# A decoder layer on one core: the last but one group's shared expert placed behind the expert tiles, and two long GpSimd instructions of each group cut in four

## The chip, the cores and the metric

The kernel runs on one core of a Trainium2 chip. The metric is the device time of one execution in microseconds (us). The core's engines are TensorE (PE in the profile, its weight loads PEld), VectorE (DVE), ScalarE (ACT), GpSimd (POOL) and SyncE (SP, which here issues DMAs).

## The reference, cut to what matters

The layer works on 32 batches of 112 tokens with 256 features, with a context of 375 rows for each batch:

```python
x = x + delta_attention(layernorm(x))            # rmsnorm, delta-rule scan over the tokens, and an MLP
x = x + cross_attention(layernorm(x), context)   # 16 heads of 16 features, mask over 375 context rows
xt = layernorm(x)                                # 3584 rows
probs = sigmoid(xt @ gate_w.T + gate_b)          # 6 experts
w, idx = top_k(probs, 2); w = w / (sum(w) + 1e-8)
y = sum over experts e:  w_e * ((silu(xt @ ew1[e].T) * (xt @ ew3[e].T)) @ ew2[e].T)
z = (silu(xt @ fc1.T) * (xt @ fc2.T)) @ fc3.T    # the shared expert, every row
x = x + y + z
```

Inside the delta attention, `h = rmsnorm(x) * norm1_w` gives queries, keys and values, and `beta = sigmoid(h @ beta_w + beta_b)`, one number for each token. Its output is `x + attn @ Wo + mlp(rmsnorm(x + attn @ Wo))`, to which the layer's own residual is added.

## The kernel before, in words

The 32 batches are worked off as eight groups (`groups`) of four (`GB = 4`); T is 112 tokens and D 256 features. A group passes three stages: the delta attention (`delta_block`, L693, and `queries`, together `ahead(g)`), the cross-attention in quads of four heads (`scores`, `turned`, `product`, then `cross_out`), and the feed-forward part with six experts. Stages of neighbouring groups are interleaved: while the quads of group g run, the delta attention of group g+1 and the feed-forward work of an earlier group fill the time between them.

**The delta attention.** `delta_block` begins with a layernorm into `h`, ScalarE making the four batches one after another. `hb = h * nwb` (L702; the profile calls its buffer `u`) is one instruction of 112x1024, on VectorE for group 0 and on GpSimd for all others; `beta` is reduced from it. Towards its end `nc.gpsimd.tensor_tensor(xt, xt, x1, ALU.add)` (L912, `x<-x,u` in the profile) adds the attention's part to the residual, again one instruction of 112x1024. Its second operand `x1` lies in a buffer with the tag `u`, which VectorE fills in two halves.

**The feed-forward part.** For groups 0 to 6, `mixture_sparse` (L1189) normalizes, turns the rows into features, computes the gate (`route`), and scatters every row twice, once for each of its two experts, into a table `rows` in DRAM (`dispatch`, `place_row`, L1144: eight indirect DMAs a group on GpSimd). It then runs the shared expert (`shared`: fc1, fc2, fc3) and stores the sum `acc` to `kept[g]`. `acc` is the group's tile `x_of[g]`. When group 6 is dispatched, `tables`, `gather` and `sparse_tiles` run the experts over 54 tiles of 128 rows: GpSimd gathers `xg` from `rows`, TensorE transposes it, multiplies up (L1327) and down (L1344), and SP stores `y` to `results` in DRAM. The last group, 7, does not pass through the tables: `mixture_dense` computes all six experts for its rows. Beside that, `combine` (L1370) finishes groups 0 to 6: for each, one load of `kept` on SP, and eight gathers from `results` on GpSimd (two for each batch), which VectorE multiplies by the weights and adds. Every gather reads `results` as a whole, so the first waits for the last store to it. The three buffers of a group in `combine` are taken in turn from nine `homes`, buffers that earlier stages have left.

**What sets the order.** The operations aren't issued at once: a `Recorder` notes them (so most have L381, the line of its replay), and its list scheduler `flush` writes out the order of TensorE, VectorE and ScalarE by hand, with costs from `price`. GpSimd and SP work off their queues in the order that this gives. Dependencies between engines are semaphores that the tile framework sets. The tail of the main function is

```python
    for _ in range(2):
        next(tiles)
    drain(out_of)
    dense = mixture_dense(groups - 1, x_of[groups - 1])
    next(dense)
    drain(tiles)
    rest = combine()
    next(rest)
    for _ in dense:
        next(rest, None)
```

In the profile `bank` is a PSUM bank, `nT` and `hT` are feature-major activations, `w_Wk` and `w_Wq` weights of the delta attention, and `mk` a buffer with this tag that also holds short-lived things, such as the copy of `rs` to 112x256.

## Time and profile before

| | us |
|---|---|
| median of 3 runs | 1423.21 |
| lowest, highest | 1422.33, 1423.34 |
| the profiled execution | 1423.09 |
| its span, first to last instruction | 1421.2 |
| outside its span | 1.9 |
| mean granted TensorE clock | 0.984 |
| TensorE busy | 1357.0 |
| VectorE busy | 970.9 |
| ScalarE busy | 704.3 |
| GpSimd busy | 308.1 |

A line of the timeline reads: start, duration, engine, line, operation, output and inputs with their shapes, and in brackets the idle time of the engine before it and what ended that. A line of a table by windows reads: the stretch and its length, then for PE, PEld, DVE, ACT and POOL the busy time with the number of instructions, then the granted clock, the share of DMA and its rate. A line of the waits names the waiting engine and buffer, the releaser, the total, the number of times and the longest.

The groups are regular: from 376.57 on, TensorE starts the same matmuls (`bank<-nT,w_Wk`) of the next group every 142 to 144 us, the last time at 946.41. The cross-attention of the last group goes on to about 1162, the tiles of the experts from 1162 to 1340, and the dense group with `combine` from there to the end.

### The profile page before, as it was taken

The page shows a single profiled execution, that of the slowest core. Times are in us where ns is not written, and L with a number is a line of the kernel's source. Part 1 is how long each engine was busy: PE and PEld are TensorE (multiplying, and loading weights), DVE is VectorE, ACT ScalarE, POOL GpSimd, SP SyncE. Part 2 cuts the span into 40 slices and gives each one's busy share as a digit, 9 for nine tenths or more (in the row PEclk, how much of TensorE's full clock was granted, in tenths as well). Part 3 has the DMA queues.
Part 4 walks back from the last instruction along what each step waited for, and adds up shares of the span by engine and source line. Part 5 has one row for each costly group of instructions (what it writes and reads, how often), then busy time and mean ns, then how long its engine had stood idle before and what let it go on. Part 6 is the DMA issues. An engine that isn't in the chain of part 4 may idle for free.

```text
span 1421.2 us, 26865 instructions
## 1 busy us (share of the span) xinstructions
PE 1357.0 (95%) x9700; PEld 919.6 (65%) x9700; DVE 970.9 (68%) x3171; ACT 704.3 (50%) x1946; POOL 308.1 (22%) x477
## 2 busy tenths in 40 slices
PE   6689999999999999999999999999999999999996
PEld 4456766776577657765776577667767666666653
DVE  6646766866886588668866786577757875455575
ACT  2124756654565456545654565466547673222110
POOL 2131000420041104100420041103110122223275
PEclk9779999999999999999999999999999999999999
DMA  9200100123012301230123012301225122222255
GB/s 259 79 8 14 35 17 17 36 69 94 17 36 69 94 17 36 69 94 16 37 69 94 17 37 68 94 17 37 61 76 163 38 64 76 85 89 84 66 169 153
DMA packets 95077, 94.76 MB, mean 67 GB/s; under 512 B 29921, under 2 KB 89057, under 8 KB 94945
## 3 DMA queue, kind: packets, MB, share of 16 engines
q1 hardware_dynamic: 86816, 72.71, 17.8%
q0 software_dynamic: 8128, 20.34, 4.8%
q8 instruction: 77, 1.26, 0.4%
q14 instruction: 56, 0.45, 0.1%
HBM read 50.90 MB, written 42.12 MB: 65 GB/s over the span
## 4 chain that ended last, share of the span: by engine, by line
PE 78%; DVE 9%; ACT 6%; issue 2%; DMA 2%; POOL 1%; POOLq 0%; DVEq 0%; ACTq 0%
PE bank L381 68%; PE bank L1327 7%; PE bank L1344 3%; ACT e L381 3%; ACT eT L381 1%; ACT h L381 1%; DVE mk L381 1%; DMA e<-results,row_i 1%; DVE W L381 1%; DVE rs_u L381 1%; DVE rs_i L381 1%; DVE ms L381 1%; DVE x L381 1%; DVE nT L381 1%; DVE qz L381 1%
## 5 line engine op out<-in xcount | busy, mean ns | idle before, releaser
L381 ACT ACTIVATE e<-e,nmx 112x375 f32<-112x375 f32 x512 | 306.2, 601 | 193.9 <-DVE nmx L381 192.8
L381 DVE CUSTOM_DVE_ANT_0 e<-bank,neg,flip 112x375 f32<-112x375 f32 x512 | 282.4, 604 | 41.5 <-PE bank L381 37.1
L381 ACT COPY eT<-bank 125x448 f32<-125x448 f32 x384 | 187.3, 529 | 90.1 <-PE bank L381 86.3
L381 PEld LDWEIGHTS bank<-ident,e 112*125 112x125 f32 x1536 | 186.6, 188 | 32.6 <-issue 9.6
L381 PE MATMUL bank<-ident,e 112*125 112x112 f32 x1536 | 201.7, 276 | 1.0 <-ACT e L381 0.7
L381 PE MATMUL bank<-kx,qz 32*112 32x375 f32 x1024 | 120.8, 518 | 0.0
L1327 PE MATMUL bank<-ew,xT 128*128 x216 | 101.9, 595 | 1.0 <-ACT e L381 1.0
L381 PEld LDWEIGHTS bank<-eT,vx 125*32 125x32 f32 x3072 | 69.2, 109 | 50.9 <-issue 37.2
L381 PE MATMUL bank<-eT,vx 125*32 125x112 f32 x3072 | 100.2, 263 | 1.3 <-DVE nT L381 1.3
L381 PE MATMUL bank<-w_xwvT,cT 128*125 128x256 f32 x384 | 100.4, 388 | 0.0
L381 DVE SCALAR_TENSOR_TENSOR hs<-hs,bank 128x256 f32<-128x256 f32 x108 | 45.4, 421 | 77.7 <-ACT hs L381 75.9
L1144 POOL DMA_INDIRECT rows<-h,row_i x56 | 52.6, 940 | 210.5 <-DMA rows<-blank 91.3
L381 ACT ACTIVATION_READ_ACCUMULATOR e<-e,nmx 112x1 f32 x512 | 96.8, 189 | 0.0
L381 PE MATMUL bank<-cT,w_xwkT 128*128 128x375 f32 x256 | 95.4, 498 | 0.0
L381 POOL DMA_INDIRECT xg<-rows,take x54 | 51.6, 955 | 130.7 <-PE bank L381 121.4
L381 ACT ACTIVATE hs<-bank 128x256 f32<-128x256 f32 x54 | 20.7, 384 | 116.2 <-PE bank L1327 113.0
L381 PEld LDWEIGHTS bank<-w_xwvT,cT 128*125 128x125 f32 x384 | 66.9, 187 | 12.0 <-issue 4.6
L381 DVE SCALAR_TENSOR_TENSOR qk<-qk,bank 128x448 f32<-128x448 f32 x56 | 34.8, 621 | 56.6 <-ACT qk L381 48.9
L381 POOL TENSOR_TENSOR u<-h,nwb 112x1024 f32<-112x1024 f32 x7 | 16.8, 2399 | 244.8 <-issue 235.3
L381 PEld LDWEIGHTS bank<-kx,qz 32*112 32x112 f32 x1024 | 40.4, 169 | 40.6 <-issue 18.7
L381 PEld LDWEIGHTS bank<-cT,w_xwkT 128*128 128x128 f32 x256 | 44.1, 190 | 33.0 <-issue 7.1
L381 DVE TENSOR_TENSOR x<-x,bank 112x512 f32<-112x512 f32 (+1 forms) x64 | 35.2, 550 | 33.5 <-PE bank L381 33.2
(245 smaller groups left out, 2406.5 us busy)
## 6 DMA issues: line engine op xcount, KB each, us to landing
rows<-blank SPq DMA_DIRECT2D x42, 448.0 KB
cT<-in_ctxT_dram SPq DMA_DIRECT2D x32, 375.0 KB
results<-y SPq DMA_DIRECT2D x54, 128.0 KB
mk<-in_mask_dram SPq DMA_DIRECT2D x32, 164.1 KB
x<-in_x_dram SPq DMA_DIRECT2D x7, 448.0 KB
kept<-x SPq DMA_DIRECT2D x7, 448.0 KB
out_dram<-x SPq DMA_DIRECT2D x4, 448.0 KB
blocks<-W SPq DMA_DIRECT2D x8, 196.0 KB
```

The lines of the kernel that those rows point to most:

```text
L381: getattr(getattr(self.nc, name), op)(*[real(a) for a in args], **{k: real(v) for k, v in kwargs.items()})
L1144: sent = rec.nc.gpsimd.indirect_dma_start(out=rows[:], out_offset=bass.IndirectOffsetOnAxis(ap=where, axis=0), in_=row, in_offset=None)
L1327: rec.nc.tensor.matmul(p.real(), xT[:, c, :], w13[:, bass.ds(at[i] * (NC * 2 * MI) + c * 2 * MI, 2 * MI)], start=(c == 0), stop=(c == NC - 1),
L1344: rec.nc.tensor.matmul(p[:, :D].real(), hT[:, c, :], w2[:, bass.ds(at[i] * (CH * D) + c * D, D)], start=(c == 0), stop=(c == CH - 1),)
```

## The change

It has three parts. First, the two GpSimd instructions of 112x1024 in `delta_block` (`hb` for groups 1 to 7, the add of `x1` for all eight) are written as four instructions of 112x256, one for each batch. Secondly, for group 6 (`groups - 2`) `mixture_sparse` issues all the scatters at once and leaves the shared expert and the store of `kept[6]` to a new function `keep_shared`, which the main function drains behind the tiles and before `combine`; the other groups run it where they did. Thirdly, because `x_of[6]` lives longer by that, the order of the `homes` is changed: the buffer with the tag `x`, first before, is now the last of the nine.

```diff
@@ delta_block
         hb = dlt.tile([T, GB, D], F32, tag="u", name=f"hb_{g}")
-        plain.tensor_tensor(hb, h, over_batches(nwb), ALU.mult)
+        if g == 0:
+            nc.vector.tensor_tensor(hb, h, over_batches(nwb), ALU.mult)
+        else:
+            for b in range(GB):
+                nc.gpsimd.tensor_tensor(hb[:, b, :], h[:, b, :], nwb, ALU.mult)
...
-        nc.gpsimd.tensor_tensor(xt, xt, x1, ALU.add)
+        for b in range(GB):
+            nc.gpsimd.tensor_tensor(xt[:, b, :], xt[:, b, :], x1[:, b, :], ALU.add)
@@ mixture_sparse
-        yield from shared(g, acc, aT, lambda: next(places, None))
+        if g == groups - 2:
+            yield from places
+            owed.append((g, acc, aT))
+        else:
+            yield from keep_shared(g, acc, aT, lambda: next(places, None))
+
+    owed = []
+
+    def keep_shared(g, acc, aT, first=lambda: None):
+        yield from shared(g, acc, aT, first)
         nc.sync.dma_start(out=kept[g].rearrange("b t d -> t b d"), in_=acc)
@@ combine
         homes = [
             pool.tile([T, GB, D], F32, tag=tag, bufs=bufs)
-            for pool, tag, bufs, n in ((io, "x", 3, 1), (att, "e", 3, 3), (att, "eT", 2, 2), (feat, "qz", 2, 2))
+            for pool, tag, bufs, n in ((att, "e", 3, 3), (att, "eT", 2, 2), (feat, "qz", 2, 2), (io, "x", 3, 1))
             for _ in range(n)
-        ] + [scratches[0].rearrange("p (b d) -> p b d", b=GB)[:T]]
+        ]
+        homes.insert(-1, scratches[0].rearrange("p (b d) -> p b d", b=GB)[:T])
@@ main
     dense = mixture_dense(groups - 1, x_of[groups - 1])
     next(dense)
     drain(tiles)
+
+    drain(keep_shared(*owed[0]))
     rest = combine()
```

## The prediction

> **What bounds the kernel now.** The page's busy totals come first, then the waits of TensorE by releaser.

> ```profile
> PE 1357.0 (95%) x9700; PEld 919.6 (65%) x9700; DVE 970.9 (68%) x3171; ACT 704.3 (50%) x1946; POOL 308.1 (22%) x477
> ...
> PE bank L381 <- DVE nT L381: 10.2, 14, 1.5
> ```

> TensorE is busy 95% of the span, so time comes from its idle gaps, from its clock, or from work behind its end. Of the 10.2 us that it waits for `nT`, five gaps of about 1.5 us are one event, once a group (376.57, 518.85, 660.80, 802.75, 946.41). The timeline around the second, on all engines:

> ```profile
> 515.28 2.41 POOL L381 TENSOR_TENSOR u<-h,nwb 112x1024 f32<-112x1024 f32 x1 [42.72 <-issue]
> 515.34 2.50 DVE L381 COPY mk<-rs 112x256 f32<-112x256 f32 x1
> ...
> 517.77 0.34 DVE L381 TENSOR_SCALAR neg<-mk 112x375 f32<-112x375 int32 x1
> 518.03 0.67 DVE L381 TENSOR_SCALAR nT<-bank,v_norm_w 128x448 f32<-128x448 f32 x1
> ```

> VectorE's copy of 112x256 takes 2.50 us here; at 339.71, with GpSimd idle, the same copy took 0.29. It ends 0.15 us after GpSimd's `u` (515.28 + 2.41 = 517.69). So a long GpSimd instruction holds VectorE, and `nT`, which TensorE needs next, stands behind the copy. [...]

> The gap also costs clock. The same eight matmuls after it, in a group of each sort:

> ```profile
> 518.85 3.25 PE L381 MATMUL bank<-nT,w_Wk 128*128 128x448 f32 x8 [1.49 <-DVE nT L381]
> ```

> ```profile
> 802.75 4.94 PE L381 MATMUL bank<-nT,w_Wk 128*128 128x448 f32 x8 [1.48 <-DVE nT L381]
> ```

> That is 1.69 us more at 802.75, and again at 946.41; the granted clock averages 0.76 in 800 to 806 and 1.00 in 516 to 522.

> The x1 add does the same to a smaller operation:

> ```profile
> 448.08 2.36 POOL L381 TENSOR_TENSOR x<-x,u 112x1024 f32<-112x1024 f32 x1 [2.56 <-ACT eT L381]
> ```

> ```profile
> 448.75 1.71 DVE L381 TENSOR_SCALAR ms<-r 112x4 f32<-112x4 f32 x1 [1.10 <-ACT h L381]
> ```

> `ms` takes 0.16 unblocked (158.59). But TensorE has other work there: its gap behind is 0.30 (456.53).

> Last the end of the span:

> ```profile
> 1343.20 0.95 POOL L381 DMA_INDIRECT e<-results,row_i  x1 [23.61 <-DVE ws L381]
> ...
> 1412.20 0.92 POOL L381 DMA_INDIRECT e<-results,row_i  x1 [0.30 <-issue]
> ```

> ```profile
> 1406.22 3.27 PE L381 MATMUL bank<-w_fc3T,hT 128*112 128x256 f32 x14 [1.03 <-DVE hT L381]
> ```

> ```profile
> 1416.08 0.48 DVE L381 SCALAR_TENSOR_TENSOR x<-e,gate,x 112x256 f32<-112x256 f32 x1 [0.27 <-DMA e<-results,row_i]
> ```

> GpSimd issues 56 gathers, one every 1.23 us, from 1343.20 to 1412.20; the first needs every store of `results`, the last of which follows the last down matmul (1338.86 to 1339.97). The last VectorE operation waits for the last gather and ends at 1416.56; a store of 4.6 us ends the span at 1421.2. TensorE ends at 1409.5 and its last add at 1410.72 + 0.68 = 1411.4. The gather chain is thus 5.2 us later than TensorE's own end.

> **Part 1a: `u` in four pieces.** The old GpSimd rows are 2.40 us for 1024 elements, 1.15 for 448 (`C`) and 0.73 for 256 (`nwb`, once). A piece is then 0.73, four with gaps of some 0.07 (estimated) 3.2 us. But a piece waits for its own batch's `h` alone, and ScalarE makes these 0.51 us apart, the last ending at 515.15; so the pieces run from about 513.75 to 516.9 instead of 517.69. The copy waits for at most a piece, and `neg` behind it for one more. If all of VectorE's four or so small operations there meet a piece each, `nT` comes only 0.2 us sooner; if none waits twice, the gap goes, 1.49. Gaps between pieces do let one short operation in: after the add of 87.08 to 89.44 `ms` ended at 89.46, and the next, `rs_i` at 89.50, took 1.05 behind the next GpSimd instruction. I take 0.8, as the pieces' end moves by that much: 5 x 0.8 = 4.0, between 1.0 and 7.4.

> **Clock.** Two drops of 1.69 followed gaps of 1.48, three such gaps had none. With gaps of 0.7 I take one drop gone, 1.7; ends 0 and 3.4. [...] The trace shows drops behind 1.48 us, and the measurement decides.

> **Part 1b: the x1 add in four pieces.** Pieces 0 and 1 need only the first half of VectorE's `u` (about 446.2), the others the second (447.65), so they end near 449.3, not 450.44, and `ms` starts at 448.75: up to 1.1 sooner, where only 0.30 of a gap is to be had. Seen from the other side, three small operations each behind a piece are later by 0.6 a group, 3.6 in six. I take +0.5 in all, ends -3.6 and +1.0.

> **Prologue.** The first two `u` (41.55, 178.14) have no such gap behind them. In the first 100 us VectorE's W chain (46.79 to 53.99, without idle) feeds TensorE's gap of 6.48 before 58.32, and `ms` its gap of 4.66 before 93.17. The add in pieces, ending 0.7 sooner, serves the second. I take 1.0, ends -1.0 and +1.4.

> **Part 2: the moved shared expert.** Its TensorE rows in the last group's attention are fc1 and fc2 at 1119.53, 1121.03, 1126.39 and 1128.00 (1.5 each) and fc3 at 1131.82 and 1141.03 (1.8 each): 9.6 us. They leave the time before the tiles (first `up` matmul 1162.00) and come back among and behind the last tiles: two fc1 runs lie before the last down matmul where the h transposes and the gate were, a net of some 0.4. So the last store of `results`, and with it all 56 gathers, would come 9.6 - 0.4 = 9.2 us sooner, if TensorE loses no more. The total of TensorE's work is the same, so its end stays at 1409.5 plus whatever idle time the move makes; call that d. The gathers then end 9.2 - d sooner, the last add of x_7 only at 1411.4 + d, and the end is 1416.0 + d: the gain is 5.2 - d, TensorE bounding.

> How large is d? The moved rows were filler for an attention in which VectorE is nearly full:

> ```profile
> 1115.00:1125.00 10.00, 9.80 (x74) 6.75 (x73) 8.30 (x32) 6.34 (x19) 0.00 (x0) 1.00 0.01 2
> 1125.00:1135.00 10.00, 9.98 (x76) 5.94 (x74) 9.14 (x38) 4.29 (x12) 5.65 (x6) 1.00 0.18 59
> 1135.00:1145.00 10.00, 10.00 (x100) 7.30 (x99) 9.62 (x36) 7.82 (x24) 1.86 (x2) 1.00 0.12 39
> 1145.00:1160.00 15.00, 14.51 (x161) 10.05 (x160) 12.48 (x49) 11.96 (x36) 3.90 (x4) 1.00 0.38 96
> ```

> The third number after the stretch's length is VectorE: 39.5 of 45 us, of which 3.8 leave with the shared expert (4 x 0.60, 2 x 0.69). 35.7 remain against 45 - 9.6 = 35.4 of TensorE: a near tie, so d is at least 0.3, and I take 0.8 for unevenness. Behind the tiles fc3 waits for VectorE's `hT`; the same step before 1406.22 cost 1.03. So d = 1.8, ends 0.5 and 6, and the gain 3.4.

> Two orders on the queues are new. The first three loads of `kept` stand at other places among the `results` stores on SP, for buffers that only the attention before the tiles reads; a store behind one of them waits for that attention's end, long past by then, so I put nothing on it. Group 6's `kept` store now stands on SP behind the last `results` store, with acc ready near 1337; the third gather set of group 2 overwrites its buffer. That set is due at 1343.20 - 7.4 + 20 x 1.23 = 1360: 20 us of cover. The scatters run in one go on GpSimd, 8 x 1.23, 10 us or more ahead of the first gather of tiles.

> **Sum.** 4.0 + 1.7 + 0.5 + 1.0 + 3.4 = 10.6. The profiled execution took 1423.09 (1421.2 and 1.9 outside), 0.1 from the median of 1423.21: 1423.1 - 10.6 = 1412.5.

> **The rivals.**
> 1. Pieces and small operations alternate strictly: 1.0 from `u`, no clock, nothing from the add or the prologue; 1423.1 - 1.0 - 3.4 = 1418.7. For it: the two rows at 89 us. Against: pieces start with each `h`, before the copy.
> 2. The tail gives nothing, d = 5.2: 1423.1 - 7.2 = 1415.9. For it: VectorE at 9.62 of 10.
> 3. Slower: without filler the last attention keeps its old length, the first `up` stays at 1162, and the shared expert is simply added behind: d = 9.6, a loss of 4.4. It decides where d exceeds 5.2 plus what the pieces bring. With their least, 1.0, the time is 1423.1 + 4.4 - 1.0 = 1426.5. For it: VectorE and ScalarE set the rhythm of scores and exponentials there. Against: VectorE loses 3.8 too, and TensorE's gaps were only 0.2 to 1.0 there.

> **How the numbers follow.** Forecast (both parts pay, 1406 to 1417) 0.58, rival 1 0.17, rival 2 0.14, rival 3 0.11. The range: with all best ends (7.4, 3.4, 1.0, 1.4, 4.7) 1405.2, so 1406 at the low end, and up to 1419 to hold rivals 1 and 2. A measurement of this kernel tells 0.2%, 2.8 us, from no change: faster 0.85 (forecast and most of rivals 1 and 2), same 0.05 (edges of rivals 1 and 3), slower 0.10.

> **What would show it.** `mk` copies near 1 us instead of 2.5 and the five gaps near 0.7 confirm 1a; runs of `w_Wk` at 3.25 after each, the clock; the first gather 7 us earlier relative to the group's start, and the last VectorE operation waiting for TensorE instead of a gather, part 2; first `up` about 7 us earlier in its group, d. I am wrong if the period from one gap to the next stays at 142 to 143.7 us, or if TensorE idles over 5 us in the last attention.

## The result, and the profile after

The changed kernel takes 1408.23 us (median of 6 runs, 1404.58 to 1409.93) beside 1422.78 for the kernel before on the same chip (6 runs, 1421.30 to 1427.04): 14.55 us less, ratio 0.9886 with a 95% interval of 0.9869 to 0.9902. The forecast was 1412.5, in a range of 1406 to 1419. The profiled execution took 1406.84, its span 1405.1.

The page's busy totals, then TensorE's waits by releaser, of the changed kernel:

```profile
PE 1354.2 (96%) x9700; PEld 920.3 (65%) x9700; DVE 958.1 (68%) x3171; ACT 703.0 (50%) x1946; POOL 315.5 (22%) x522
```

```profile
PE bank L381 <- DVE nT L381: 5.4, 14, 1.4
```

VectorE has the same 3171 instructions and is busy 12.8 us less (970.9 before): that much less waiting lies inside its instructions. TensorE's waits for `nT` fell from 10.2 to 5.4 us.

The event of the second group, in the changed kernel's timeline on GpSimd, VectorE and TensorE:

```profile
512.40 2.94 POOL L381 TENSOR_TENSOR u<-h,nwb 112x256 f32<-112x256 f32 x4 [40.24 <-ACT h L381]
```

```profile
514.83 0.66 DVE L381 COPY mk<-rs 112x256 f32<-112x256 f32 x1
515.42 0.34 DVE L381 TENSOR_SCALAR neg<-mk 112x375 f32<-112x375 int32 x1
515.68 0.67 DVE L381 TENSOR_SCALAR nT<-bank,v_norm_w 128x448 f32<-128x448 f32 x1
```

```profile
937.06 3.25 PE L381 MATMUL bank<-nT,w_Wk 128*128 128x448 f32 x8 [0.44 <-DVE nT L381]
```

The copy takes 0.66 instead of 2.50, and the gap before `w_Wk` is 0.44 or 0.45 in all five groups instead of 1.47 to 1.49. All five runs of `w_Wk` take 3.25; the two of 4.94 are gone. The early pieces have a price that the gap already contains: they hold two operations `a` of VectorE's layernorm, which took 0.73 us together before.

```profile
512.42 1.63 DVE L381 TENSOR_SCALAR a<-x,bmv,rstd 112x256 f32<-112x256 f32 x2
```

Behind the x1 add, VectorE's `ms` and TensorE's transposes, after:

```profile
448.48 0.48 DVE L381 TENSOR_SCALAR ms<-r 112x4 f32<-112x4 f32 x1 [1.10 <-ACT h L381]
```

```profile
455.70 0.93 PE L381 MATMUL bank<-ident,h 112*128 112x112 f32 x8
456.46 1.04 PE L381 MATMUL bank<-ident,e 112*125 112x112 f32 x8
```

and the transposes before, where the eighth had a line to itself:

```profile
455.97 0.26 PE L381 MATMUL bank<-ident,h 112*128 112x112 f32 x1
456.53 1.50 PE L381 MATMUL bank<-ident,h 112*128 112x112 f32 x7 [0.30 <-ACT h L381]
```

Eight transposes take 0.93 us when nothing holds them; before, the eight lasted from 455.97 to 458.03, which is 2.06 us. Three of the seven in the last line waited for ScalarE's `h`. Only the first idle time of a run is in brackets; the others lie inside its duration.

The tail, after:

```profile
1323.75 0.93 POOL L381 DMA_INDIRECT e<-results,row_i  x1 [24.25 <-issue]
...
1392.77 0.92 POOL L381 DMA_INDIRECT e<-results,row_i  x1 [0.30 <-issue]
```

```profile
1396.58 3.28 PE L381 MATMUL bank<-w_fc3T,hT 128*112 128x256 f32 x14 [1.67 <-DVE hT L381]
```

```profile
1399.90 0.69 DVE L381 TENSOR_TENSOR x<-x,bank 112x512 f32<-112x512 f32 x1 [1.04 <-PE bank L381]
```

The last VectorE operation now waits for TensorE (`PE bank`), not for a gather; VectorE has finished with the last gathered rows at 1396.0, 3.9 us ahead of it.

TensorE issues its matmuls in the same order in both kernels up to 1119 us, so start times can be compared one by one. The difference of the two spans, 16.1 us, splits so (us, gain positive):

| where | gain | forecast |
|---|---|---|
| five gaps before `w_Wk`, 1.04 each | 5.2 | 4.0 |
| half-clock `w_Wk` runs at 802.75 and 946.41 | 3.35 | 1.7 |
| transposes behind `ms`, groups 2 to 7: 0.82 to 1.13 each | 5.3 | 0.5 |
| given back where TensorE waits for later `h` | -0.8 | 0 |
| first 110 us | -1.2 | 1.0 |
| from 1119 us to the end | 4.2 | 3.4 |
| sum | 16.05 | 10.6 |

These are two single executions; the medians differ by 14.55.

### The profile page after: what moved, and what is told of

It reads as the page before. It is cut to its first block, busy times and chain, and to the rows that moved or that the text cites. A ratio compares the mean times of both kernels' runs of the same rounds, so it can differ in the third digit from the quotient of the medians.

```text
span 1405.1 us, 26935 instructions
## 1 busy us (share of the span) xinstructions
PE 1354.2 (96%) x9700; PEld 920.3 (65%) x9700; DVE 958.1 (68%) x3171; ACT 703.0 (50%) x1946; POOL 315.5 (22%) x522
## 4 chain that ended last, share of the span: by engine, by line
PE 82%; DVE 7%; ACT 4%; DMA 3%; issue 2%; POOL 1%; DVEq 0%; POOLq 0%; ACTq 0%
PE bank L381 72%; PE bank L1341 7%; PE bank L1358 3%; ACT e L381 2%; ACT eT L381 1%; DVE W L381 1%; DMA e<-results,row_i 1%; POOL e L381 1%; DMA qz<-results,row_i 1%; DVE nT L381 1%; DVE qz L381 1%; DVE a L381 1%; DVE x L381 1%; DMA x<-results,row_i 1%; DVE rs_i L381 0%
## 5 line engine op out<-in xcount | busy, mean ns | idle before, releaser
L381 ACT ACTIVATE e<-e,nmx 112x375 f32<-112x375 f32 x512 | 306.2, 601 | 176.7 <-DVE nmx L381 175.5
L381 DVE CUSTOM_DVE_ANT_0 e<-bank,neg,flip 112x375 f32<-112x375 f32 x512 | 282.5, 604 | 38.5 <-PE bank L381 34.2
L381 ACT COPY eT<-bank 125x448 f32<-125x448 f32 x384 | 187.1, 528 | 84.8 <-PE bank L381 80.6
L381 PEld LDWEIGHTS bank<-ident,e 112*125 112x125 f32 x1536 | 186.9, 189 | 34.9 <-issue 10.1
L381 PE MATMUL bank<-ident,e 112*125 112x112 f32 x1536 | 203.0, 276 | 1.7 <-ACT e L381 0.9
L381 PE MATMUL bank<-kx,qz 32*112 32x375 f32 x1024 | 121.7, 519 | 0.0
L381 PEld LDWEIGHTS bank<-eT,vx 125*32 125x32 f32 x3072 | 69.2, 109 | 50.5 <-issue 36.9
L381 PE MATMUL bank<-eT,vx 125*32 125x112 f32 x3072 | 100.2, 263 | 1.4 <-DVE nT L381 1.3
L381 PE MATMUL bank<-w_xwvT,cT 128*125 128x256 f32 x384 | 100.4, 388 | 0.0
L381 DVE SCALAR_TENSOR_TENSOR hs<-hs,bank 128x256 f32<-128x256 f32 x108 | 45.5, 421 | 78.2 <-ACT hs L381 76.2
L381 ACT ACTIVATION_READ_ACCUMULATOR e<-e,nmx 112x1 f32 x512 | 96.9, 189 | 0.0
L381 PE MATMUL bank<-cT,w_xwkT 128*128 128x375 f32 x256 | 95.7, 498 | 0.0
L381 ACT ACTIVATE hs<-bank 128x256 f32<-128x256 f32 x54 | 20.7, 383 | 119.6 <-PE bank L1341 116.4
L381 POOL DMA_INDIRECT xg<-rows,take x54 | 51.5, 954 | 119.5 <-PE bank L381 108.2
L381 PEld LDWEIGHTS bank<-w_xwvT,cT 128*125 128x125 f32 x384 | 66.9, 188 | 12.0 <-issue 4.6
L381 DVE SCALAR_TENSOR_TENSOR qk<-qk,bank 128x448 f32<-128x448 f32 x56 | 34.8, 621 | 57.1 <-ACT qk L381 49.4
L381 POOL TENSOR_TENSOR u<-h,nwb 112x256 f32<-112x256 f32 x28 | 20.6, 767 | 232.5 <-ACT h L381 232.5
L381 PEld LDWEIGHTS bank<-kx,qz 32*112 32x112 f32 x1024 | 41.2, 170 | 40.6 <-issue 15.0
L381 PEld LDWEIGHTS bank<-cT,w_xwkT 128*128 128x128 f32 x256 | 44.1, 190 | 32.9 <-issue 7.2
L381 DVE TENSOR_TENSOR x<-x,bank 112x512 f32<-112x512 f32 (+1 forms) x64 | 35.4, 552 | 39.1 <-PE bank L381 38.5
```

What stands on the lines that cost most here:

```text
L381: getattr(getattr(self.nc, name), op)(*[real(a) for a in args], **{k: real(v) for k, v in kwargs.items()})
```

## The experiments

The theory: a GpSimd instruction holds some VectorE instructions for its whole length (in the kernel before, the copy took 2.50 us beside a `u` of 2.41), so what matters is how long one such instruction is; and the tail gained because the chain of gathers starts sooner. The rivals are named in the expectations. Each kernel was timed against the kernel before on its own chip.

### The three parts alone

Each is the kernel before with one hunk of the change: the `hb` pieces (`u_only`), the x1 pieces (`x_only`), or `owed`, `keep_shared` and the new order of `homes` (`tail_only`).

> Only the hb multiply is cut in four. Theory (a GpSimd instruction holds VectorE's short instructions for its whole length, so a piece holds them for a quarter): the copies mk behind it take 0.66 us instead of 2.50 and the five gaps of TensorE before w_Wk are 0.45 instead of 1.49, 5 x 1.04 = 5.2 us; with the two half-clock intervals of 1.7 us gone or not, 5.2 to 8.6 in all: 1414.5 to 1418. Rival (the three parts pay only together, because each alone leaves the other's wait as the next bound): under 3 us, above 1420.

> Only the x1 add is cut in four. Theory (VectorE's ms is held for 1.4 us by the add, and three transposes in a row behind it each wait for ScalarE's h): about 0.8 to 1.1 us in each of groups 2 to 7, 5.0 in all, the five gaps of 1.49 stay: about 1418. Rival (only the listed gap of 0.30 is to be had, as the prediction took it): 0.5 us, about 1422.5.

> Only the shared expert of group 6 is moved, with the order of homes; both GpSimd instructions whole. Theory (the end was set by the 56 gathers, 5.2 us behind TensorE's own end, and is now set by TensorE): the first gather some 7.6 us sooner, 3 to 4.5 us in all: about 1419. Rival (VectorE, held by whole GpSimd instructions, makes the last attention longer without the filler): 0 to 1 us, about 1422.5.

Ratios 0.9936 (0.9914 to 0.9957), 0.9928 (0.9907 to 0.9950) and 0.9988 (0.9972 to 1.0005). On this chip, though, every kernel took longer: the one before 1464.21. The tail accounts for it. In `u_only`, whose tail is the old one, TensorE stood still for 17.76 us (13.65 to 19.89 as the longest time in the other three kernels of this chip):

```profile
1394.64 1.20 PE L381 MATMUL bank<-ew,hT 128*112 128x256 f32 x2 [17.76 <-DVE hT L381]
```

and VectorE's longest waits there were listed with the releasers "remote" (15.23) and "issue" (9.65). What held them was not found. The part before 1119 us is as on the first chip, and there the traces answer: in `u_only` the five gaps are 0.42 to 0.45, each 1.03 to 1.06 below the trace of before; in `x_only` the five gaps stay (1.46 to 1.49) and TensorE gains 0.71 to 1.13 at the transposes of each of six groups, 5.2 in all. The listed gap of 0.30 was not the measure. The tail stayed open, so all three were run again on other chips.

> The kernel of u_only once more, for a time with an undisturbed tail. Theory: five gaps of 0.45, 5 x 1.04 = 5.2 us less 0.1 us given back at the next stage of each group; with the half-clock intervals as they fall, 4 to 8.5 us below the kernel before. Rival: as in the first run.

> The kernel of x_only once more, for a time with an undisturbed tail. Theory: 0.8 to 1.1 us in each of six groups as in the first trace, 5.2 us in all, give or take a half-clock interval of 1.7: 3.5 to 7 us below the kernel before. Rival (the listed gap of 0.30 alone): 0.5 us.

> The kernel of tail_only once more. In the first run TensorE, VectorE and ScalarE stood still for 14 to 18 us at a time in the tail, in this kernel and in those with the old tail alike, so the tail measured something else. Theory: where the tail runs undisturbed, as in the two profiles of before and after, the first gather comes about 7.6 us sooner, TensorE's end bounds, and the time falls by 3 to 4.5 us. Rival: nothing, as in the first run (ratio 0.9988).

`u_only_b`: 1416.23 against 1425.46, ratio 0.9935 (0.9921 to 0.9950). `x_only_b`: 1417.48 against 1425.46, 0.9939 (0.9923 to 0.9955). `tail_only_b`: 1421.70 against 1426.78, 0.9972 (0.9958 to 0.9985), 5.1 us. The first gather of `tail_only_b` starts 7.6 us sooner by the alignment on TensorE's starts (0.46 later than before at 1119):

```profile
1336.07 0.93 POOL L381 DMA_INDIRECT e<-results,row_i  x1 [24.24 <-issue]
```

and its span is 3.4 shorter from there, with TensorE bounding the end. So each part pays alone: 9.2, 8.0 and 5.1 us by the medians. They add up to 22.3, and the whole change brought 14.55 on its first chip and 18.3 on the chip of `tail_only_b`. One part of that is counted twice: the first 110 us, where `u_only_b` and `x_only_b` each gain 1.2 us in their traces. The half-clock intervals, of which more below, fall differently in every kernel; how much of the difference is theirs was not shown.

### Shorter holds, or an earlier start?

The pieces of `hb` also start sooner, each with its own batch's `h`. In `u_cols` the kernel before gets pieces that can't:

```diff
+            for c in range(4):
+                at = slice(c * (D // 4), (c + 1) * (D // 4))
+                nc.gpsimd.tensor_tensor(hb[:, :, at], h[:, :, at], over_batches(nwb[:, at]), ALU.mult)
```

> The hb multiply is cut in four by columns: each piece takes 64 columns of all four batches, so each waits for the last h as the whole did, and the last ends no sooner than the whole, 517.7 or later in the second group with a gap; the rest as before the change. Theory (what matters is how long one instruction holds VectorE): copy and the operation behind it wait for one piece each, nT at about 517.0, gaps of 0.4 to 0.9: 3 to 5.5 us less, and more if the half-clock intervals go: 1414.5 to 1420. Rival (the pieces pay because each starts with its own batch's h, and so the work ends sooner): gaps of 1.5 to 2, 1423 or more.

Ratio 0.9944 (0.9924 to 0.9964). The timeline of `u_cols` in the same group, GpSimd, VectorE, TensorE:

```profile
519.82 3.01 POOL L381 TENSOR_TENSOR u<-h,nwb 112x256 f32<-112x256 f32 x4 [42.51 <-issue]
```

```profile
519.88 0.84 DVE L381 COPY mk<-rs 112x256 f32<-112x256 f32 x1
520.64 0.90 DVE L381 TENSOR_SCALAR neg<-mk 112x375 f32<-112x375 int32 x1
521.45 0.67 DVE L381 TENSOR_SCALAR nT<-bank,v_norm_w 128x448 f32<-128x448 f32 x1
```

```profile
522.27 3.25 PE L381 MATMUL bank<-nT,w_Wk 128*128 128x448 f32 x8 [0.38 <-DVE nT L381]
```

GpSimd's work ends at 522.83, 0.6 us later after its start than the whole instruction, and yet the gap is 0.38 (0.35 to 0.38 in all five groups). The copy waits for one piece (0.84, where it took 0.29 with GpSimd idle), `neg` for the next (0.90 instead of 0.34), and `nT`, which reads PSUM, for none (0.67 as before), though a third piece runs beside it. So strict alternation of pieces and small operations, the forecast's first rival, does take place; it costs little because only two such operations stand ahead of `nT`. The early start is not what pays: in the changed kernel the pieces are over sooner, so `neg` waits for none (0.34), but they have held the two operations `a` instead (1.63 where 0.73 is enough). Why the copy and `neg` are held and `nT` is not was not shown.

### Finer pieces

`u_eight` is the changed kernel with `hb` in eight pieces of 112x128; `both_eight` cuts the x1 add in eight as well.

> The changed kernel with the hb multiply in eight pieces of 112x128 instead of four of 112x256. Theory (a short VectorE instruction waits for at most one piece, and two stand ahead of nT): a piece is about 0.46, so the five gaps of 0.45 shrink to 0.1 to 0.4, but eight pieces last about 1.1 us longer than four: between 2 us faster and 1 us slower than the changed kernel. Rival (the fixed part of each piece, 0.18 us by the fit, and more turns cost VectorE more): gaps of 0.8 or more, 2 us slower or worse.

`u_eight` took 1404.89 against 1426.78, ratio 0.9848 (0.9828 to 0.9869), where the changed kernel had 0.9876 (below) on the same chip: 3.6 us less by the medians, with intervals that overlap. Its eight pieces last 3.66 us and still leave TensorE almost no wait (0.12 before `w_Wk`):

```profile
513.35 0.52 DVE L381 COPY mk<-rs 112x256 f32<-112x256 f32 x1
513.80 0.61 DVE L381 TENSOR_SCALAR neg<-mk 112x375 f32<-112x375 int32 x1
```

```profile
515.14 3.25 PE L381 MATMUL bank<-nT,w_Wk 128*128 128x448 f32 x8
```

A group is 0.43 us shorter than in the changed kernel, 2.1 us over the five gaps; the remaining 1.5 is within what half-clock intervals move, 1.69 for one run of `w_Wk` (the profiled execution of the changed kernel had one at 43 us, that of `u_eight` one at 123).

> The changed kernel with both GpSimd instructions in eight pieces of 112x128, the fastest version that the theory points to. Theory: the gaps of u_eight (about 0.1 before w_Wk, 0.43 us a group less than the changed kernel), and VectorE's ms, 0.47 behind a quarter, falls to 0.2 to 0.35, of which at most 0.1 to 0.3 us a group reaches TensorE: 2 to 4.5 us faster than the changed kernel. Rival (more pieces last longer and give back what they free): as the changed kernel or slower than u_eight.

1405.36 against 1425.46, 0.9861 (0.9845 to 0.9878). Against its own `old_homes` (below, 0.9885) it is 3.4 us faster; against `u_eight`, a group is equally long in the traces (2.19 and 2.18 below the kernel before). In these traces cutting the add finer brings nothing. `u_eight` and `both_eight` have the lowest medians here, with intervals that overlap those of the changed kernel.

### The tail: an earlier chain, or a shorter attention?

`shared_before_tiles` is the changed kernel with the drain moved:

```diff
     drain(out_of)
+    drain(keep_shared(*owed[0]))
     dense = mixture_dense(groups - 1, x_of[groups - 1])
     next(dense)
     drain(tiles)
-    drain(keep_shared(*owed[0]))
```

> The changed kernel, but the shared expert of group 6 is drained ahead of the tiles instead of behind them; the scheduler puts it among the middle tiles, so the attention is as short as with the change, but the last store of results comes about 9 us later than with it. Theory (the gain is that the chain of 56 gathers starts sooner): the first gather 8 to 9 us later than in the changed kernel and the gathers bound the end again: about 4 us slower than the changed kernel. Rival (the gain came from taking the shared expert out of an attention that was full): as fast as the changed kernel.

1414.39 against 1426.78, 0.9917 (0.9900 to 0.9935): 5.9 us slower than the changed kernel on the same chip. Of that, 4.8 us lie behind 1119 us in the two traces. The first gather starts 8.8 us later than in the changed kernel (12.1, less the 3.3 by which the two traces differ at 1119), and the end waits for the last gather again, while TensorE ends at 1402.2:

```profile
1335.83 0.94 POOL L381 DMA_INDIRECT e<-results,row_i  x1 [23.61 <-issue]
```

```profile
1408.47 0.48 DVE L381 SCALAR_TENSOR_TENSOR e<-e,gate,e 112x256 f32<-112x256 f32 x1 [0.20 <-DMA e<-results,row_i]
```

The whole gain of the tail is gone, though the attention is as short as with the change: from the matmul that starts at 1119 us in the kernel before, its first `up` follows 37.8 us later, as in the changed kernel, and 42.5 us later in the kernel before. The gain came from the earlier chain.

### The order of `homes`, and the changed kernel again

> The changed kernel with the order of homes as before, so that the first load of kept goes into the buffer of group 6 and waits behind the store of its sum. Theory (TensorE bounds the end; the load comes some 3 us after the store at 1328, VectorE starts its multiplications about 6 us later and catches up in 60 us): 0 to 1 us slower than the changed kernel. Rival (the third part is needed for the gain of the second): 3 us slower or worse.

1408.81 against 1425.46, 0.9885 (0.9866 to 0.9904), as the changed kernel; from 1119 us on its trace gains 4.1 us, as with the new order. The third part of the change brings nothing and costs nothing measurable.

> The changed kernel again, as the reference for the other three on one chip. Theory: five gaps near 0.45 before w_Wk whatever the phase of the clock's half-speed intervals; these fall elsewhere than in the first profile, with the prologue's loss of 1.2 us there or not. Rival: the half-speed interval at 43 us belongs to the change and is there again.

1408.48 against 1426.78, 0.9876 (0.9854 to 0.9898). The gaps are 0.44 to 0.46. The half-clock interval at 43 us was there again, but it is not the change's: `x_only` and `u_cols` have one there too, `u_eight`, `old_homes` and `both_eight` do not.

## Why the prediction was right, point by point

The sign held, the median lies in the range, and the mechanisms of `u` and of the tail held. The size was a quarter too small by the medians, and the term of the x1 add failed. That the sum still fell into the range is in part luck: two terms lay outside their own ends, the x1 add 4.3 us above its best, and, in the profiled execution, the prologue 0.2 us below its worst.

- **`u` in pieces.** Right in kind. The gap shrank by 1.04 where 0.8 was taken, between the two ends. The reason given for 0.8, that the pieces end 0.8 sooner, was wrong: in `u_cols` they end later, and the gap is as short. What counts is how long the operations ahead of `nT` are held: copy and `neg` took 2.84 us together before and 1.74 in `u_cols`; with the two `a` they took 3.57 before and 2.63 in the changed kernel. The 0.07 put between pieces was an estimate: in the changed kernel four pieces follow each other without a gap, 2.94 us in all where 3.2 was taken.
- **Clock.** One of two half-clock runs was taken as gone; both went. In the nine traces with `u` in pieces none of the 45 gaps, 0.46 at most, was followed by a half-clock run of `w_Wk`; in the five traces with `u` whole 7 of 25 gaps were, and in `x_only` none of five. By that an execution with `u` whole has 1.4 such runs on the average, worth 2.4 us, and the two in the profile of before were more than that. In the windows below, TensorE is busy for 2.81 to 2.93 of 3.41 us with a gap of 0.45, and for 1.92 to 2.03 with one of 1.48 or 1.49.
- **The x1 add.** The largest miss: 0.5 taken, 5.3 measured. The step that failed is "where only 0.30 of a gap is to be had". 0.30 was the first idle time of a run of seven transposes of which three waited for ScalarE's `h`; the eight took 2.06 us where 0.93 is enough, and the difference of 1.13 was to be had in that group. The other end of the term, three small operations that each wait for a piece, was not seen: behind `ms` (0.48) the next take 0.17.
- **Prologue.** Forecast 1.0, measured -1.2 in the profiled execution, mostly because `w_Wk` at 43 us ran at half clock (4.97 us). In `u_only_b`, `x_only_b`, `old_homes` and `both_eight`, without that interval, TensorE stands 0.95 to 1.28 us ahead of the kernel before at 110 us, so 1.0 was about right there, and in `u_eight` and `shared_before_tiles` 0.64 and 0.82; but `u_only`, without it too, stands 0.33 behind, and the kernels without pieces scatter by 0.3 to 0.5 at this point, so the term is not measured closely.
- **The tail.** The first gather came 7.6 us sooner (forecast 7.4), d was 2.2 (1.8) by TensorE's end, and the gain 4.2 (3.4). The difference is a term that the sum lacked: before, the last add started 1.2 us behind TensorE's end because VectorE was multiplying gathered rows, and now it starts at once. In `tail_only_b`, `after_again` and `u_eight` the same stretch gained 3.4 to 3.8 us with d of 2.6 to 3.0. The parts of d agree less well than their sum. By the forecast's own 9.2 us, 1.6 of d arose before the first gather, where 0.8 was taken, and 0.6 behind it, where 1.0 was taken. The first `up`, named as the sign of d with about 7 us, came only 4.7 sooner; yet TensorE's idle time ahead of it did not grow (1.7 us before, 1.1 after). The scheduler put products of the attention (24 more of `eT,vx`, 8 more of `kx,qz`) ahead of it that had run beside the tiles, so this sign did not measure d.
- **The rivals.** Alternation is real and cheap (copy 0.84, `neg` 0.90, gap 0.38 in `u_cols`). TensorE's end loses 2.2 to 3.0 us (d) by the move, far from the 5.2 at which that would have eaten the gain; as its idle time in the attention did not grow, it is not shown that missing filler is the cause. The new wait of the third set of gathers on the `kept` store was never seen.

## What to carry to other kernels

Where one engine's instruction holds another engine, as GpSimd's hold VectorE's here, look at how long *one* instruction is, not at its total: cutting it cost the holding engine a little here (GpSimd 308.1 to 315.5 us), and each held operation of the other then waited for one piece (the copy took 0.66 us, 0.84 in `u_cols`, instead of 2.50). When reading a gap from a merged row, compare the row's duration with the same row undisturbed; the bracket shows only the first idle time. Where two engines end within a few microseconds of each other, a move gains the distance between them and no more, so work out both ends.

## What the runs showed of the hardware

```profile
373.06:376.47 3.41, 2.03 (x17) 1.16 (x17) 3.40 (x4) 1.66 (x3) 2.36 (x1) 1.00 0.00 0
516.42:519.83 3.41, 1.92 (x11) 1.15 (x8) 3.41 (x7) 0.81 (x3) 1.27 (x1) 1.00 0.17 48
799.72:803.14 3.42, 1.94 (x15) 1.09 (x14) 3.42 (x5) 1.18 (x3) 1.88 (x1) 1.00 0.06 7
943.08:946.50 3.42, 1.93 (x18) 1.10 (x16) 3.42 (x4) 1.47 (x3) 2.17 (x1) 1.00 0.00 0
```

The last two were followed by 3.41 us at half clock, the first two were not: here the edge lay at some 1.9 us busy of 3.41. It wasn't a sharp one. In the five traces with `u` whole, windows 1.91 to 1.97 us busy went either way, and none from 1.99 to 2.63, which hold the gap whole or in part, was followed by a drop. In the changed kernel the same place:

```profile
934.15:937.56 3.41, 2.81 (x20) 1.63 (x20) 3.38 (x8) 1.84 (x4) 1.76 (x3) 1.00 0.10 14
```

With 2.8 to 2.9 us busy (2.81 here, 2.93 in the other four groups) none dropped in the two traces of the changed kernel. Intervals that come and go with the phase of this grid would fit the spread among the executions of one kernel (5.7 and 8.3 us for the kernel before on two chips, 5.35 for the changed one) and the mean granted clock beside it (in `after_again` 0.989 for the shortest, 1404.42, and 0.983 for the longest, 1411.21); that they cause it was not shown. One place stays open: nine intervals, in eight of the fourteen traces (at 564.8 in `tail_only_b`, at 280.5 and 983.6 in `shared_before_tiles`, and in `old_homes`, `both_eight`, `u_cols`, `u_only_b`, `x_only` and `x_only_b`), followed windows that were 3.20 us busy. Each of the nine windows holds all sixteen gate matmuls of a group, of six columns each, beginning 1.40 to 1.69 us into the window. In groups 0 to 5, the groups of the nine, no window that holds all sixteen at another place (39 of them, up to 1.24 us or from 1.86) was followed by an interval; in the last two groups, where other operations stand beside the gate, none was at 1.59 to 1.65 either. So the phase of the grid goes with it here too, but the busy time that the profile shows does not tell these windows from others; which of their operations count for less, if any do, was not tried.

**Operations of VectorE that read PSUM were not held** beside GpSimd pieces: in the changed kernel ten `qz` (0.67 to 0.68 us) and seven `u<-a,bank` (0.69 us) that overlap pieces last as long as those that do not (0.68, and 0.68 to 0.69), whereas `ms`, 112x4 elements from SBUF, which takes 0.16 undisturbed, was held for 1.25 to 1.55 us by the whole add of the kernel before (1.41 to 1.71) and for 0.3 by a piece (0.45 to 0.48).
